# Per-pair starting steps and work splits in a four-layer image network kernel

## The chip, the cores and the metric

The kernel runs on one core of one Trainium2 chip. Such a core has TensorE (PE, matmuls into PSUM), VectorE (DVE), ScalarE (ACT, table functions), GpSimd (POOL, elementwise, SBUF only) and SyncE (SP, which here issues all DMAs). Each engine runs its own queue strictly in the order in which it was written; engines wait for each other through semaphores. The metric is the device time of one execution in microseconds (us).

## The reference

The input is x of shape (8, 384, 32, 32) in fp32. Four residual layers follow one another, each with a group norm (32 groups) ahead:

```python
x = x + L0(gn(x))   # Mamba: in_proj 384->2x768, causal conv 3, silu, x_proj, dt_proj + softplus,
                    #   h = exp(dt*A)*h + dt*u*B ; y = sum_n h*C + D*u   (16 states, 1024 positions)
                    #   y * silu(z), out_proj 768->384
x = x + L1(gn(x))   # 1x1 matmul, 8x8 FFT filter, 3x3 depthwise, gelu(x1)*x2, 1x1 matmul
x = x + L2(gn(x))   # layer norm over channels, Mamba as in L0, then MLP 384->1536 gelu ->384
x = x + L3(gn(x))   # 3x3 depthwise convolution
```

The scan is the heart: for 768 channels and 16 states a first-order recurrence over 1024 positions, in two layers and eight images.

## The kernel before

An image of 1024 positions is cut into two chunks of 512. There are 32 chunks: 0 to 15 belong to layer 0 (two per image), 16 to 31 to layer 2. Even chunks begin an image, odd ones end it. A chunk has 24 steps (NQ): six groups of 128 channels, each in four substeps. In a step 128 partitions hold 16 states times 8 channels, and four blocks j of 512 positions make 32 channels. All the work is counted in steps; the step at which chunk n begins is `s["t"] = 24 n`.

What one step does, by process (lines of the kernel before):

- `begins` (777): SP loads g, the product dt*u spread over the states (1 MB in SBUF, tag g, five buffers), and every fourth step dts. The load for step t waits until PE has gathered step t-5.
- `times` (800): POOL multiplies g (128x2048) by B.
- `decays` (810) and `exps` (825): PE spreads dt into the PSUM tiles dA, ACT turns each into exp(dt*A).
- `scans` (833): DVE runs four scans. SHARE says how many of the four blocks are scanned into dA rather than into g. For these DVE also makes the product with C (`g<-dA,bc`); for the others POOL does it in `states` (881), `g<-g,bc` on 128x1024 at a share of 2.
- `carries` (859): in even chunks only, ACT copies the last column of each block, the state with which the odd chunk starts. POOL's C product and PE's next dA wait for that.
- `gathers` (894): PE sums over the states into y; `gatings` (917): DVE multiplies y by silu(z).

Around the steps run jobs of whole chunks, which use PE, ACT and DVE between them: `front` (621) makes the next chunk's u, B, C and dt (blocks of in_proj with the convolution on DVE, a Silu, `step` for dt and its softplus, `scaled` for dt*u on POOL); `gates` (575) makes z in two halves; `finish` (937) makes out_proj, in layer 2 followed by `mlp` (1201). `layer1` (1069) and `layer3` (1266) do the convolution layers of an image while later chunks scan; they are added once the image's odd chunk has ended. In `layer3` PE does TAPS (4) of the nine taps of each block by diagonal matrices and DVE the other five (`ps_dw<-xp,vec,ps_dw`).

All 32 chunks are one program, unrolled in Python. The order on each queue is made by `Order` (194), a list scheduler: processes are generators that name the engine they need next; `Clocks` (68) estimates when the engine is free and the operands are there; the process that can begin earliest goes next. Among those that can begin at once the scan's processes go first on PE, ACT and SP; after that the lower `due`, a step, wins on PE, POOL and SP, and on DVE and ACT the one ready longest. So `due` is a preference. A hard floor is `pace(t)` (292): the process may not go on before the written scans reach step t. Conv blocks of `front` are paced at `s["t"] - 18 + d`, dt at `s["t"] - 9 + 3*d`, layer 1's patches at steps 8, 13, 18 and 23 of the even chunk after the image, its depthwise sums at 28 and 38, layer 3's taps at 20 and every 7 from there.

ACT needs another table for Silu and Gelu than for Exp and Ln. Such calls are gathered: `session` (563) holds them until LEAD (2) exponentials more than scans are written, or until PATIENCE (6.0) has passed on the scheduler's clock. A session is a table load, the function, a table load back.

Every recorded operation has line 189 in the profile, so groups are told apart by tile names.

Of the kernel before, what the change touches and what calls it, by code (L numbers as in the profile page):

```python
# [19 lines left out]
KC = C // P  # L20
# [26 lines left out]
NBANK = 3  # L47
LEAD = 2
PATIENCE = 6.0
TAPS, LAST_TAPS = 4, 5  # L50
SHARE = (2, 2, 2, 2)
SET_EXP = "natural_log_exp_and_others"
# [11 lines left out]
def _img(ap):  # L64
    return ap.rearrange("p (h w) -> p h w", w=W)


# [182 lines left out]
def tile_conv_preact_d4(ctx: ExitStack, tc: tile.TileContext, a: dict, out: bass.AP):  # L250
# [41 lines left out]
    def pace(t):  # L292

        return once(lambda: ahead["scans"] >= 4 * min(t, len(steps)))
# [268 lines left out]
    def session():  # L563

        asked = []

        def ready():
            asked.append(order.now)
            late = order.now - asked[0] > PATIENCE
            late = late or ("begin", ahead["decays"] // 4) not in said  # L570
            return 0.0 if ahead["decays"] - ahead["scans"] >= LEAD or late or order.stuck else None

        return ready

    def gates(s, h):
        n = s["n"]
        yield once(lambda: "normed" in s and "loaded" in s["w"] and (n == 0 or chunks[n - 1]["gated"] >= (NH if h == 0 else ND)))
        z = s["z", h] = new(wk, [P, NH, T], F32, "z", 2)

        def block(d):  # L580
            ps, tag = yield from projection(s, "ps_z", "z", (h * NH + d) * P)
            yield on("ACT", ps)
            act(z[:, d, :], ps, AF.Copy)
            ps_give(ps, tag)

        yield from together(s["t"] + (6 if h else -4), [block(d) for d in range(NH)])
        yield on("ACT", z, when=session())
        act(_flat(z), _flat(z), AF.Silu)
        exp_set()
        s["gates", h] = True  # L590
# [30 lines left out]
    def front(s):  # L621
        c, n, due = s["c"], s["n"], s["t"] - 26
        yield once(lambda: n == 0 or "normed" in chunks[n - 1] and (n == 1 or ("gates", 1) in chunks[n - 2]))
# [21 lines left out]
        def block(d):  # L645
            if n not in (0, B * NCH - 1, B * NCH):
                yield pace(s["t"] - 18 + d)
            ps, tag = yield from projection(s, "ps_in", "in", d * P)
            yield on("ACT", ps)
            act(u[d], ps, AF.Identity, scale=vec[:, d, 2:3], bias=vec[:, d, 3:4])  # L650
            if c < NCH - 1:
                act(s["xt"][:, d, :], ps[:, T - 2 : T], AF.Copy)
            for j in (1, 2):
                yield on("DVE", u[d])
                vector.scalar_tensor_tensor(
                    u[d][:, j:T], ps[:, 0 : T - j], vec[:, d, 2 - j : 3 - j],
                    u[d][:, j:T], ALU.mult, ALU.add,
                )
            ps_give(ps, tag)
# [38 lines left out]
        def step(d):  # L698
            if n not in (0, B * NCH - 1, B * NCH):
                yield pace(s["t"] - 9 + 3 * d)  # L700
            ps, tag = yield from chain(
# [26 lines left out]
            else:  # L728
                yield on("POOL", pc[:, 0, :])
                gpsimd.tensor_sub(m, v, pc[:, 0, :])  # L730
                rest, tag = m, None
            order.add(scaled(d, v), s["t"] - 14)
            yield on("ACT", rest)
# [31 lines left out]

    ahead = {"decays": 0, "scans": 0}
    said = {}

    def seen(*keys):


        def ready():
            return None if any(k not in said for k in keys) else 0.0

        return ready

    def begins():
# [32 lines left out]
    def decays():  # L810
        for t, (s, i) in enumerate(steps):
            k, sub = QUADS[i]
            for j in range(4):
                procs["decays"]["due"] = t - 2
                yield on("PE", when=lambda: (
                    None if ("begin", t) not in said or t > 0 and (
                        ("scan" if j < 4 - SHARE[(i - 1) % NSUB] else "product", t - 1, j) not in said
                        or j > 0 and not carried(t - 1, j)
                    )
                    else max(clocks.known(s["dts"][k]), clocks.last.get(dAs[j].name, 0.0))  # L820
                ))
                mm(dAs[j], selr[:, j, :], s["dts"][k][:, sub, :])
                said["decay", t, j] = True
# [9 lines left out]
    def scans():  # L833
        for t, (s, i) in enumerate(steps):
            for j in range(4):
# [4 lines left out]
                g = s["g", i]  # L840
                low = 4 - SHARE[i % NSUB]
                q = 4 * i + j
# [16 lines left out]
    def carries():  # L859
        for t, (s, i) in enumerate(steps):  # L860
            if s["c"] == NCH - 1:
                continue
            low = 4 - SHARE[i % NSUB]
            yield on("ACT", when=lambda: (
# [11 lines left out]
    def carried(t, j):  # L876
        s, i = steps[t]
        low = 4 - SHARE[i % NSUB]
        return s["c"] == NCH - 1 or ("carry", t, j) in said or 0 < j < low

    def states():
        for t, (s, i) in enumerate(steps):
            low = 4 - SHARE[i % NSUB]
            procs["states"]["due"] = t + 0.3
# [52 lines left out]
    def finish(s):  # L937
        n, t = s["n"], s["t"]
        last = s["pre"] == "l2_"
        due = t + NQ + (10 if not last else 23 if s["c"] == 0 else 16)  # L940
        end = n == len(chunks) - 1
# [50 lines left out]

        yield from together(t + NQ + 6, [block(m) for m in range(KC)])
        s["free"] = True
# [73 lines left out]

    def layer1(s):
        b, due = s["b"], s["t"] + (NQ + 14 if s["n"] == B * NCH - 1 else 3 * NQ - 14)  # L1070
        x = [chunks[s["n"] - 1]["x"], s["x"]]
# [9 lines left out]
        for hb in range(H // PS):  # L1081
            if not hurry:
                yield pace(s["t"] + NQ + 8 + 5 * hb)
            xl = new(p1, [P, KC, 2, P], F32, "xl")
# [38 lines left out]
        for hf in range(2):  # L1123
# [22 lines left out]
            if not hurry:  # L1146
                yield pace(s["t"] + NQ + 28 + 10 * hf)
            yield from depthwise(p1, P, "ps_dw", due, [some(0), some(2)])
# [117 lines left out]
    def layer3(s):  # L1266
        b, due = s["b"], s["t"] + 3 * NQ - 1
        x = [chunks[s["n"] - 1]["x"], s["x"]]
# [22 lines left out]
        taken = [0]  # L1291
        taps = LAST_TAPS if end else TAPS
        for k in range(KC):
# [7 lines left out]
            for hf in range(2):  # L1301
                yield pace(s["t"] + NQ + 20 + (7 if b < B - 2 else 4) * (2 * k + hf))
                rows = slice(hf * 512, (hf + 1) * 512)
# [31 lines left out]
    chunks = [  # L1335
        {"pre": pre, "src": src, "b": b, "c": c, "n": (q * B + b) * NCH + c, "gated": 0}
        for q, (pre, src) in enumerate((("l0_", a["x"]), ("l2_", x_mid)))
# [7 lines left out]
    def start_jobs(t):  # L1345
        n, i = divmod(t, NQ)
        if i or n >= len(chunks):
            return
        s = chunks[n]
        order.add(gates(s, 1), t + 8)  # L1350
        if s["c"] == 0 and n + NCH < len(chunks):
            m = chunks[n + NCH]
            order.add(measured(m), t + NQ + 4)
        if n + 1 < len(chunks):
            later = chunks[n + 1]
            order.add(front(later), t + NQ - 26)
            order.add(gates(later, 0), t + NQ - 4)
        order.add(finish(s), t + NQ + 10)
# [178 lines left out]
```

## Time and profile before

| | us |
|---|---|
| median of 3 runs (6209.75 to 6211.98) | 6210.31 |
| profiled execution | 6204.07 |
| its span, first to last instruction | 6202.2 |
| start to the first scan | 74.4 |
| layer 0, odd chunks 5, 7, 9, 11, 13 | 169.3 each |
| layer 0, even chunks 4, 6, 8, 10, 12 | 185.3 to 192.6 |
| layer 2, chunks 20 to 29, odd / even | 198.3 to 199.4 / 187.0 to 188.4 |
| chunk 17, the longest | 218.4 |
| after the last scan | 120.7 |

A chunk's time is from its first scan to the next chunk's first scan. In a group's line the engine stands first, then the operation, the tile written and those read, shapes, the count, and behind the bar the busy time, the mean of one in ns, and the engine's idle time ahead of these instructions with what ended it. An fp32 matmul is recorded as two passes, so its count is doubled. Records of matmuls overlap: their pace is the distance of their starts, not their length.

### The profile page before, as it was taken

How to read it: one execution, taken by the hardware profiler on the slowest of the kernel's cores; microseconds unless marked ns; L12 is line 12 of the kernel's file. 1: busy time of each engine (PE TensorE's matmuls, PEld its weight loads, DVE VectorE, ACT ScalarE, POOL GpSimd, SP SyncE). 2: the span in 40 equal slices, each digit the busy share in tenths (PEclk: the TensorE clock that was granted, in tenths of full speed). 3: DMA queues.
4: the chain of work that ended last, by engine and by line, in shares of the span. 5: the costliest groups of instructions: out<-in, count | busy, mean ns of one | idle time of the engine just before them, and what ended most of it. 6: DMA issues, size and time to landing. Idle time of an engine off the chain costs nothing.

```text
span 6202.2 us, 62614 instructions
## 1 busy us (share of the span) xinstructions
PE 5799.2 (94%) x19022; PEld 2184.1 (35%) x19022; DVE 5616.8 (91%) x6381; ACT 4241.3 (68%) x7942; POOL 5725.3 (92%) x2028
## 2 busy tenths in 40 slices
PE   6878999999999999999989999999999999999998
PEld 2223333333333333333333333333333333333333
DVE  5999999999998999998887899899998999989994
ACT  5656677677667767776676676777767777677753
POOL 4999999999999999989997999999999999999991
PEclk8889999999999999999999999999999999999999
DMA  6877878877887888787777888878888788888871
GB/s 178 193 184 186 195 190 194 204 188 193 190 193 185 196 205 189 192 205 186 180 185 183 199 196 219 200 198 209 198 215 201 200 207 198 212 205 197 207 197 58
DMA packets 346724, 1195.88 MB, mean 193 GB/s; under 512 B 40516, under 2 KB 142580, under 8 KB 248084
## 3 DMA queue, kind: packets, MB, share of 16 engines
q1 hardware_dynamic: 346388, 1191.88, 79.1%
q8 instruction: 152, 2.49, 0.2%
q14 instruction: 184, 1.51, 0.1%
HBM read 1040.73 MB, written 150.99 MB: 192 GB/s over the span
## 4 chain that ended last, share of the span: by engine, by line
DVE 25%; PE 13%; POOL 8%; DMA 4%; issue 4%; ACT 4%; SPq 0%; POOLq 0%; DVEq 0%; ACTq 0%
DVE g L189 11%; DVE dA L189 8%; POOL g L189 6%; DVE u L189 2%; PE ps_dn L189 2%; PE ps_up L189 2%; PE ps_dw L189 2%; PE y L189 2%; PE dA L189 2%; DMA g<-dud 2%; DVE ps_dw L189 1%; PE ps_z L189 1%; DMA dts<-dtd 1%; PE ps_out L189 1%; DVE st L189 1%
## 5 line engine op out<-in xcount | busy, mean ns | idle before, releaser
L189 POOL TENSOR_TENSOR g<-g,bc 128x1024 f32<-128x1024 f32 (+1 forms) x1536 | 5243.4, 3447 | 248.1 <-ACT carry L189 94.1
L189 ACT ACTIVATE dA<-dA,w_A 128x512 f32<-128x512 f32 x3072 | 2018.6, 661 | 931.0 <-PE dA L189 919.4
L189 PE MATMUL dA<-dts,selr 96*128 96x512 bf16 x3072 | 1190.0, 390 | 233.2 <-DVE g L189 207.6
L189 DVE TENSOR_TENSOR_SCAN g<-dA,carry,g 128x512 f32<-128x512 f32 x768 | 955.4, 1269 | 75.1 <-POOL g L189 61.1
L189 DVE TENSOR_TENSOR g<-dA,bc 128x512 f32<-128x512 f32 x1536 | 994.5, 677 | 17.3 <-ACT carry L189 16.4
L189 DVE TENSOR_TENSOR_SCAN g<-dA,g 128x512 f32<-128x512 f32 x768 | 909.4, 1209 | 85.7 <-POOL g L189 77.8
L189 DVE TENSOR_TENSOR_SCAN dA<-dA,carry,g 128x512 f32<-128x512 f32 x768 | 952.2, 1271 | 28.0 <-ACT dA L189 27.4
L189 DVE TENSOR_TENSOR_SCAN dA<-dA,g 128x512 f32<-128x512 f32 x768 | 909.0, 1212 | 62.3 <-ACT dA L189 61.7
L189 PE MATMUL y<-g,sely 128*32 128x512 f32 x6144 | 857.0, 627 | 38.0 <-POOL g L189 35.6
L189 PEld LDWEIGHTS <-selr 96*128 96x128 bf16 x3072 | 300.2, 98 | 1113.0 <-issue 1072.0
L189 PE MATMUL ps_in<-xf,w_in 128*128 128x512 f32 x1152 | 562.7, 610 | 10.0 <-ACT xf L189 7.6
L189 PE MATMUL ps_z<-xf,w_z 128*128 128x512 f32 x1152 | 567.8, 597 | 3.6 <-DVE dt L189 3.6
L189 PE MATMUL ps_up<-t,mw 128*128 128x512 f32 x1152 | 556.0, 596 | 7.1 <-DVE u L189 5.2
L189 PE MATMUL ps_out<-u,w_out 128*128 128x512 f32 x1152 | 547.5, 594 | 0.4 <-ACT carry L189 0.4
L189 PE MATMUL ps_dn<-h,mw 128*128 128x512 f32 x1152 | 545.3, 594 | 1.6 <-ACT h L189 1.6
L189 PE MATMUL ps_dw<-tp,diag 128*128 128x512 f32 x864 | 438.8, 609 | 9.6 <-ACT diag L189 9.6
L189 PEld LDWEIGHTS y<-g,sely 128*32 128x32 f32 x6144 | 126.3, 109 | 599.2 <-issue 313.0
L189 PEld LDWEIGHTS ps_in<-xf,w_in 128*128 128x128 f32 x1152 | 218.6, 195 | 263.8 <-issue 234.2
L189 POOL TENSOR_TENSOR dt<-dt,u 128x512 f32<-128x512 f32 x192 | 244.3, 1274 | 72.4 <-PE ps_dr L189 56.3
L189 PEld LDWEIGHTS ps_dn<-h,mw 128*128 128x128 f32 x1152 | 217.8, 190 | 259.9 <-issue 235.3
L189 PEld LDWEIGHTS ps_up<-t,mw 128*128 128x128 f32 x1152 | 214.4, 190 | 267.2 <-issue 230.4
L189 PEld LDWEIGHTS ps_z<-xf,w_z 128*128 128x128 f32 x1152 | 215.9, 191 | 252.7 <-issue 215.2
(118 smaller groups left out, 6451.1 us busy)
## 6 DMA issues: line engine op xcount, KB each, us to landing
g<-dud SPq DMA_DIRECT2D x768, 1024.0 KB, 8.2
dtd<-pc SPq DMA_DIRECT2D x192, 384.0 KB, 4.0
dts<-dtd SPq DMA_DIRECT2D x192, 384.0 KB, 7.8
mw<-in_l_mlp_w SPq DMA_DIRECT2D x192, 384.0 KB, 6.5
dud<-dt SPq DMA_DIRECT2D x768, 64.0 KB, 3.2
xf<-in_x SPq DMA_DIRECT2D x16, 768.0 KB, 9.1
x<-in_x SPq DMA_DIRECT2D x16, 768.0 KB, 11.9
x_mid<-x SPq DMA_DIRECT2D x16, 768.0 KB, 7.0
```

The source lines that it names most:

```text
L189: return call(out_, *args, **kw)
```

## The change

The constants LEAD, PATIENCE, TAPS and SHARE and the numbers in the paces and dues become a table WAYS of 18 named values with alternatives, the first of each being the value of before. CHOICE holds one number per chunk, the same for both chunks of a pair, which `ways` turns into one alternative for every name. When a chunk's first step comes up, `start_jobs` puts that chunk's values into `way`. `front` of the next chunk, `finish` of this one and the layers added during it read a copy; sessions read it as it stands; the share stays with the chunk, since its scans, carries and C products must agree.

Decoded, what differs from before:

| chunks | values |
|---|---|
| 0, 1 | share (2,2,2,3), out 2, begin -24 |
| 2, 3 | out 2, begin -28 |
| 4 to 7 | patch_every 4, out 2, begin -28 |
| 8, 9 | the same, lead 1 |
| 10, 11 | the same, lead 2, dt_every 2.5, early -1 |
| 12, 13 | patch_every 4, out 2, begin -28, lead 3 |
| 14, 15 | patch_every 4, out 10, begin -28, lead 3 |
| 16, 17 | share (2,3,2,2) |
| 18, 19 | dt_every 2.5, wait 9 |
| 20, 21 | dt -10, dt_every 2.5, wait 9 |
| 22, 23 | lead 3, wait 4, share (2,3,2,2) |
| 24, 25 | dt -10, dt_every 2.5, taps 3, wait 9, share (2,2,2,1) |
| 26, 27 | dt -8, dt_every 2.5, taps 3, wait 9, share (2,2,2,1) |
| 28, 29 | as before |
| 30, 31 | dt -10, taps 3, wait 9, share (2,2,2,1) |

(A value "tap" is also set in chunks 2 to 15, where no layer 3 reads it.) "out" is the due of out_proj, 6 before; "begin" that of `front`, -26 before. "early" is the due of the first half of z, -4 before; "lead" and "wait" stand for LEAD and PATIENCE. Share 3 in a substep leaves POOL a C product of 128x512 there, share 1 one of 128x1536. Taps 3 leaves PE three taps and gives DVE six; layer 3 of an image reads it when it is added, in the even chunk after the image, so it reaches three images. Operations are otherwise the same in kind and number; conv, patch and sums starts other than patch_every keep their values.

```diff
-LEAD = 2
-PATIENCE = 6.0
-TAPS, LAST_TAPS = 4, 5
-SHARE = (2, 2, 2, 2)
+LAST_TAPS = 5
+WAYS = {
+    "lead": (2, 1, 3),
+    "conv": (-18, -20, -16),
+    "dt": (-9, -10, -8),
+    "dt_every": (3, 2.5, 2),
+    "patch": (8, 5, 11),
+    "patch_every": (5, 4),
...
+    "out": (6, 2, 10),
+    "mlp": (0, -6, 6),
+    "wait": (6.0, 4.0, 9.0),
+    "begin": (-26, -24, -28),
+    "scaled": (-14, -18, -10),
+    "share": ((2, 2, 2, 2), (2, 2, 2, 3), (2, 3, 2, 2), (2, 2, 2, 1)),
+}
+CHOICE = (
+    96013674, 96013674, 19490544, 19490544, 19495161, 19495161, 19495161, 19495161, 19495162,
...
+def ways(number):
+
+    chosen = {}
+    for name, values in WAYS.items():
+        number, digit = divmod(number, len(values))
+        chosen[name] = values[digit]
+    return chosen
...
-            late = order.now - asked[0] > PATIENCE
+            late = order.now - asked[0] > way["wait"]
...
-                yield pace(s["t"] - 18 + d)
+                yield pace(s["t"] + o["conv"] + d)
...
-                yield pace(s["t"] - 9 + 3 * d)
+                yield pace(s["t"] + o["dt"] + o["dt_every"] * d)
...
+    def share(t):
+        s, i = steps[t]
+        return s["share"][i % NSUB]
...
-                low = 4 - SHARE[i % NSUB]
+                low = 4 - share(t)
...
-        yield from together(t + NQ + 6, [block(m) for m in range(KC)])
+        yield from together(t + NQ + o["out"], [block(m) for m in range(KC)])
...
-                yield pace(s["t"] + NQ + 8 + 5 * hb)
+                yield pace(s["t"] + NQ + o["patch"] + o["patch_every"] * hb)
...
-        taps = LAST_TAPS if end else TAPS
+        taps = LAST_TAPS if end else o["taps"]
...
+        way.update(ways(CHOICE[n]))
         s = chunks[n]
+        s["share"] = way["share"]
...
-            order.add(front(later), t + NQ - 26)
+            order.add(front(later), t + NQ + way["begin"])
```

## The prediction

> **What bounds the kernel now.** I read the totals first, then stretches of the span cut at the first scan of each chunk (VectorE runs 96 scans per chunk, so the cuts are exact), then GpSimd's waits in one stretch, then prices by form of instruction.
>
> ```profile
> PE 5799.2 (94%) x19022; PEld 2184.1 (35%) x19022; DVE 5616.8 (91%) x6381; ACT 4241.3 (68%) x7942; POOL 5725.3 (92%) x2028
> ```
>
> Three engines are over 90% busy, so no single one can be relieved alone. The stretches show which binds where. Columns: us, then busy us of PE, weight loads, DVE, ACT, POOL, then the granted clock, DMA share, GB/s. The five are chunks 9 and 10 (layer 0), then 25, 26 and 30 (layer 2).
>
> ```profile
> 1696.00:1865.30 169.30, 164.50 (x561) 61.78 (x558) 164.95 (x181) 116.51 (x211) 168.64 (x54) 1.00 0.82 196
> 1865.30:2057.90 192.60, 175.37 (x603) 66.55 (x602) 173.09 (x206) 136.94 (x297) 176.49 (x63) 0.95 0.79 189
> ...
> 4729.80:4928.60 198.80, 193.13 (x620) 72.84 (x618) 188.48 (x214) 137.56 (x220) 187.01 (x69) 1.00 0.82 202
> 4928.60:5115.60 187.00, 182.86 (x599) 69.30 (x600) 175.09 (x202) 137.41 (x267) 182.93 (x71) 1.00 0.85 207
> ...
> 5700.30:5884.60 184.30, 177.47 (x583) 66.88 (x584) 172.02 (x195) 134.39 (x259) 182.65 (x71) 1.00 0.85 205
> ```
>
> Odd chunks of layer 0 are POOL and nothing else: 169.30 - 168.64 = 0.66 us idle. Even ones have 192.60 - 176.49 = 16.1 us of POOL idle: the largest stock of waits that repeats (12.0 to 16.1 us in chunks 4 to 12). Layer 2 is bound by PE: 4.1 us idle in chunk 26, 5.7 in chunk 25, while POOL has 4.1 and 11.8. What POOL waits for in chunk 10, and its worst wait:
>
> ```profile
> POOL g L189 <- ACT carry L189: 7.6, 4, 3.0
> POOL g L189 <- DMA g<-dud: 5.9, 4, 4.0
> POOL dt L189 <- ACT z L189: 1.2, 1, 1.2
> POOL g L189 <- DVE g L189: 1.0, 1, 1.0
> ```
> ```profile
> 1971.14 2.36 POOL L189 TENSOR_TENSOR g<-g,bc 128x1024 f32<-128x1024 f32 x1
> 1977.54 6.84 POOL L189 TENSOR_TENSOR g<-g,bc 128x2048 f32<-128x2048 f32 x2 [4.04 <-DMA g<-dud]
> ```
>
> A load of g may go out only when PE has gathered the step five before. Going through POOL's written order, I count by how many steps its B product (128x2048) runs ahead of its C product (128x1024) at each issue. Of 768 issues 88 stand three ahead; these hold 49.6 of the 76.8 us that POOL waits for g in the whole run. In chunks 6, 8, 10 and 12 the waits of 4.0 to 4.5 us sit at such places, steps 15 and 16.
>
> One table session of ScalarE (Silu or Gelu between the Exps) blocks that engine for 4.1 us; after this one POOL waited 3.0 us for a carry:
>
> ```profile
> 1920.10 1.28 ACT L189 ACT_TABLE_LOAD   x1
> 1921.39 1.49 ACT L189 ACTIVATE z<-z 128x1536 f32<-128x1536 f32 x1
> 1922.89 1.28 ACT L370 ACT_TABLE_LOAD   x1
> ```
>
> **Prices.** In the groups by form the mean ns stands after the busy time; the line of the timeline below them gives PE's pace.
>
> ```profile
> L189 POOL TENSOR_TENSOR g<-g,bc 128x2048 f32<-128x2048 f32 x768 | 3479.6, 4535 | 90.5 <-DMA g<-dud 76.5 <-PE dA L189 3.3 <-PE ps_dn L189 3.1
> ...
> L189 POOL TENSOR_TENSOR g<-g,bc 128x1024 f32<-128x1024 f32 x768 | 1810.9, 2359 | 157.7 <-ACT carry L189 94.1 <-DVE g L189 59.2 <-PE dA L189 3.1
> ...
> L189 DVE TENSOR_TENSOR g<-dA,bc 128x512 f32<-128x512 f32 x1536 | 994.5, 677 | 17.3 <-ACT carry L189 16.4
> ...
> L189 DVE SCALAR_TENSOR_TENSOR ps_dw<-xp,vec,ps_dw 128x512 f32<-128x512 f32 x210 | 154.9, 738 | 14.1 <-PE ps_dw L189 13.7
> ```
> ```profile
> 3360.94 5.31 PE L189 MATMUL ps_dn<-h,mw 128*128 128x512 f32 x12
> ```
>
> A C product of one block moved from DVE to POOL costs POOL (4535 - 2359)/2 = 1.09 us and frees 0.68 of DVE. An fp32 matmul is two passes; twelve took 5.31 us, the last recorded as 0.59, so a pass is (5.31 - 0.59)/11 = 0.43 and a matmul 0.86 us.
>
> **The change part by part.** No transfer is added; 36 blocks go from POOL to DVE and 36 back, 18 matmuls go from PE, 18 operations come to DVE. The rest is order. The sum is made against the profiled execution: 6204.1 us, span 6202.2 and 1.9 around it. The median of the runs stands 6.2 above it.
>
> *Chunks 0 and 1, share 3 in every fourth step.* Twelve blocks leave POOL: -13.1 us; DVE gets 12 x 0.68 = +8.1. POOL idles 15.4 and 5.0 us in these chunks, DVE 28.1 and 12.8, PE more. Between -13.1 (POOL binds throughout) and +8.1 (DVE does), POOL is nearest to full, but part of its idle time is the start's: **-8**.
>
> *Chunks 2 and 3.* POOL idles 9.1 us, of which waits for g 6.5, at steps 7, 8, 15 and 17. Bounds 0 and -9.1; the order is milder but not free of threes: **-3**.
>
> *Chunks 4 to 13: out-projection four steps earlier in the order of preference, patches every 4 steps instead of 5, front two steps earlier, lead 1 or 3 in some.* The written orders show three things. Threes on POOL fall from 30 to 8, and those at steps 13 to 16, where the 4 us waits are, become twos (not in chunk 12). In chunks 6 to 13 one z session per pair leaves the even chunk (5 to 4) for the odd one (3 to 4), where no carry stands behind it. And in chunks 6 to 9 twelve patch matmuls move from the odd to the even chunk and three z matmuls back; at 0.86 us or less each that is under 8 us for PE, which idles 17 there. Per pair that is up to 5.1 us of g waits and about 3.0 of carry wait. What is late next: three ahead means DVE's scans were behind, so part of the freed time becomes waiting for scans. SP issues the same loads in another order; xf goes out two steps earlier on the same queue as g, covered only if g is not late. Bounds per pair: 0, and -14.4 (all POOL idle of chunks 4 to 13 is 72 us in five pairs). I take -5, about the g waits alone: **-25**.
>
> *Chunks 14 and 15.* POOL idles 26.9 us, PE 33.9, DVE 48.6: nobody binds. Two sessions leave, one joins chunk 16. Bounds 0 and -27; as a pair before it: **-5**.
>
> *Chunks 16 to 19.* Shares take 13.1 us off POOL, add 8.1 to DVE. Ten matmuls, 8.6 us, leave chunk 17's part of PE's queue, eight of them down-projections to chunk 18; 17 is the longest chunk (218.4 us), 18 has 8.7 us of PE idle. Bounds -8.6 and +8.1; PE binds more than DVE there: **-5**.
>
> *Chunks 20 to 23.* PE idles 5 us a chunk and its work is the same; dt starts one step earlier, every 2.5. Bounds 0 and -10 a pair: **-3** for both.
>
> *Chunks 24 to 31, share 1 and three taps.* The taps apply to three images: 18 matmuls off PE, -15.5 us; 18 x 0.738 = +13.3 on DVE, from which 36 products, 24.4 us, go; POOL gets 36 x 1.09 = +39.2, 13.1 a pair. In chunks 25 and 26 POOL works 369.9 of 385.8 us; with 13.1 more it needs 383.0. So relief of 5.2 us on PE is worth at most 385.8 - 383.0 = 2.8, and with POOL's present waits kept (15.9) the pair gets 13.1 longer. Chunk 30 alone, at 182.65 busy, would need 189.2 against 184.3. Ends for three pairs: -15.5 and +39; with waits halfway between the odd layer-0 chunks' 0.66 and today's the pair is near even, and the tail behind the last scan keeps its work: **0**.
>
> A rule to weigh: the Trainium skill, Perfetto Trace Analysis, section Identifying the Most-Contended Engine, says that matmul busy share tells little of TensorE's headroom and that the weight loads' busy share should be read. In chunk 26 that is 69.30/187.0 = 37%, so by it PE would have room, the 18 matmuls would be worth nothing, and the sum would be 13 us higher. The trace's gapless passes 0.43 us apart speak for PE being full, and I keep them.
>
> Sum: -8 - 3 - 25 - 5 - 5 - 3 + 0 = -49. 6204.1 - 49 = 6155; on the median 6210.3 - 49 = **6161 us**.
>
> **The rivals.**
>
> *The waits only change their name.* With POOL no longer ahead it waits for scans; DVE idles 16.5 to 19.5 us in chunks 6 to 12, partly for other reasons (a dA product of PE comes 4.2 us late for ScalarE at 1935.1 us). Then pairs give -1 instead of -5 and the rest half: -5 - 12 = -17, about 6193. For it: carry waits, 7.6 us in chunk 10, exceed the g waits.
>
> *New load waits (slower).* Every engine's queue is fixed when the program is written, and the real landing of g (median 8.2 us, a chain piece of 15.79 at 5498.86) is not in it. If the new order puts one wait of 4.0 us into each chunk that lacks one: eleven chunks now have a wait for g of 2.5 us or more, so 21 would gain 4.0 = +84, against -49, which gives 6245. It cancels the gain at 12 new waits and decides from 16. Against it: threes fall from 88 to 64.
>
> *Nearly all goes.* Both the g and carry waits leave the five pairs (-13 each) and the rest stands: -49 - 40 = -89, 6121. Against it: even chunks still keep four sessions.
>
> *The shares overload POOL.* If the pairs 24 to 27 and 30/31 pay the whole 39, the sum is -10: 6200, no change.
>
> **How the numbers follow.** No change means within 0.2%, 12.4 us. Forecast (-30 to -70) 0.42; name only (-13 to -30) 0.16; nearly all 0.10; shares, or gains that cancel, within 12 us: 0.11; new load waits 0.21. Faster 0.42 + 0.16 + 0.10 = 0.68, same 0.11, slower 0.21. The low end, 6118, cuts half of "nearly all"; the high end, 6240, cuts about half of the slow case. With gain alone the range would be 6140 to 6180.
>
> **What would show it.** Right: even chunks 6 to 12 about 185 us instead of 189 to 193, with no 4 us wait for g at step 15; odd ones still near 169; chunk 17 shorter; chunk 24 and 30 not shorter, POOL at full there. Wrong: new waits of POOL for g or carry in odd chunks of layer 0, or pairs of 24 to 31 longer by over 6 us.

## The result, and the profile after

The median went from 6210.86 us (six runs, 6204.84 to 6213.29) to 6179.53 us (six runs, 6168.05 to 6182.48): a ratio of 0.9948 with a 95% interval of 0.9935 to 0.9961, so 31 us or half a per cent faster. The profiled execution after took 6178.5 us with a span of 6176.7, 25.5 less than the span before.

The totals of the page after differ little from those of before. PE has 18 matmuls fewer (36 records) and is busy 24.7 us less, DVE is busy 13.6 us more, POOL 3.1 us less:

```profile
PE 5774.5 (93%) x18986; PEld 2186.5 (35%) x18986; DVE 5630.4 (91%) x6399; ACT 4232.4 (69%) x7924; POOL 5722.2 (93%) x2028
```

POOL's idle time fell by 22.4 us and DVE's by 39.1; PE's stayed (403.0 and 402.2). So what was gained is idle time of POOL and DVE between their instructions. Cut at the first scan of each chunk, the difference of the two spans comes out like this (us):

| chunks | before | after | difference | term of the prediction |
|---|---|---|---|---|
| start | 74.4 | 73.5 | -0.9 | |
| 0, 1 | 364.5 | 375.6 | +11.1 | -8 |
| 2, 3 | 354.3 | 348.7 | -5.6 | -3 |
| 4 to 13 | 1793.1 | 1783.6 | -9.5 | -25 |
| 14, 15 | 392.3 | 367.0 | -25.3 | -5 |
| 16 to 19 | 791.6 | 787.0 | -4.6 | -5 |
| 20 to 23 | 772.0 | 768.6 | -3.4 | -3 |
| 24 to 31 and the tail | 1660.0 | 1672.6 | +12.6 | 0 |

In chunks whose order was the same in several of the kernels below, a pair's time differs by 2 to 5 us from one execution to the next, so the single pairs are read no finer than that. Chunks 4 to 13 together took 1793.1 to 1800.1 us in the five profiles that have the order of before there (mean 1796.3), and 1781.1 to 1783.6 in the three that have the order of the change (mean 1782.3): by the means they gained 14.0 us, not 9.5. For chunks 0 and 1 and for 14 and 15 the means differ from the table by 1.1 us at most.

Stretches of the span after, one per line. The columns are us, then busy us of PE, weight loads, DVE, ACT and POOL, then granted clock, DMA share, GB/s. They are chunks 0 and 1, 7 and 8, 14 and 15:

```profile
73.50:267.80 194.30, 145.57 (x428) 43.38 (x427) 163.13 (x186) 113.07 (x233) 170.41 (x61) 0.79 0.82 194
267.80:449.10 181.30, 144.54 (x456) 45.75 (x455) 167.61 (x185) 104.70 (x163) 169.87 (x57) 0.85 0.81 188
1337.00:1515.10 178.10, 169.86 (x552) 62.08 (x553) 164.18 (x180) 120.36 (x206) 175.67 (x56) 0.96 0.79 189
1515.10:1695.30 180.20, 168.86 (x608) 67.93 (x607) 172.98 (x207) 134.03 (x302) 169.21 (x61) 0.98 0.83 198
2581.40:2765.80 184.40, 171.26 (x591) 66.63 (x589) 174.72 (x207) 137.27 (x296) 177.30 (x64) 0.96 0.87 208
2765.80:2948.50 182.70, 171.93 (x590) 66.32 (x591) 167.72 (x181) 130.53 (x237) 179.06 (x63) 1.00 0.83 193
```

The same view of the kernel before, for its chunks 7 and 8:

```profile
1337.10:1506.40 169.30, 164.49 (x561) 61.78 (x558) 164.95 (x182) 116.50 (x211) 168.64 (x54) 1.00 0.82 196
1506.40:1696.00 189.60, 172.30 (x603) 65.45 (x602) 172.85 (x205) 136.80 (x297) 176.42 (x63) 0.96 0.79 190
```

The even chunk 8 became 9.4 us shorter, and the odd chunk 7 8.8 us longer. POOL's busy time went the same way: 168.64 to 175.67 in chunk 7, 176.42 to 169.21 in chunk 8. Its idle time in the two was 0.66 + 13.18 = 13.8 us and is now 2.43 + 10.99 = 13.4. Work was moved across the cut, and little else happened.

What POOL waited for in chunks 4 to 13, before and then after (us in total, times, longest):

```profile
POOL g L189 <- ACT carry L189: 32.7, 17, 3.8
POOL g L189 <- DMA g<-dud: 24.9, 16, 4.5
POOL g L189 <- DVE g L189: 3.8, 6, 1.0
```
```profile
POOL g L221 <- ACT carry L221: 47.0, 25, 3.9
...
POOL g L221 <- DVE g L221: 2.3, 4, 0.7
POOL g L221 <- DMA g<-dud: 1.7, 2, 1.5
```

The waits for g did go, nearly all of them (24.9 to 1.7 us). Waits for carries rose by 14.3, and the ten chunks gained 9.5 (14.0 by the means). Over the whole run the same exchange shows: POOL's waits for g fell from 76.8 to 52.6 us, and its waits for carries rose from 94.1 to 118.8.

### The profile page after: what moved, and what is told of

The parts are those of the page before. It is cut to its first block, busy times and chain, and to the rows that moved or that the text cites. A ratio compares the mean times of both kernels' runs of the same rounds, so it can differ in the third digit from the quotient of the medians.

```text
span 6176.7 us, 62588 instructions
## 1 busy us (share of the span) xinstructions
PE 5774.5 (93%) x18986; PEld 2186.5 (35%) x18986; DVE 5630.4 (91%) x6399; ACT 4232.4 (69%) x7924; POOL 5722.2 (93%) x2028
## 3 DMA queue, kind: packets, MB, share of 16 engines
HBM read 1040.73 MB, written 150.99 MB: 193 GB/s over the span
## 4 chain that ended last, share of the span: by engine, by line
DVE 19%; PE 18%; POOL 17%; issue 8%; ACT 7%; DMA 4%; SPq 0%; POOLq 0%; DVEq 0%; ACTq 0%
POOL g L221 15%; DVE g L221 9%; DVE dA L221 6%; DMA g<-dud 3%; PE y L221 3%; PE ps_dw L221 3%; PE ps_dn L221 2%; PE dA L221 2%; PE ps_up L221 2%; ACT dA L221 2%; DVE u L221 1%; PE ps_in L221 1%; PE ps_z L221 1%; POOL dt L221 1%; DVE ps_dw L221 1%
## 5 line engine op out<-in xcount | busy, mean ns | idle before, releaser
L221 POOL TENSOR_TENSOR g<-g,bc 128x2048 f32<-128x2048 f32 (+3 forms) x1536 | 5241.8, 3448 | 241.5 <-ACT carry L221 118.8
L221 DVE TENSOR_TENSOR g<-dA,bc 128x512 f32<-128x512 f32 x1536 | 994.7, 679 | 16.9 <-ACT carry L221 15.7
L221 DVE SCALAR_TENSOR_TENSOR u<-ps_in,w_vec,u 128x511 f32<-128x511 f32 (+1 forms) x384 | 279.8, 732 | 28.8 <-ACT xt L221 17.0
## 6 DMA issues: line engine op xcount, KB each, us to landing
x<-in_x SPq DMA_DIRECT2D x16, 768.0 KB, 11.7
```

The costliest lines, as they stand in the source:

```text
L221: return call(out_, *args, **kw)
```

## The experiments

### Parts of the change alone

Four kernels take a part of the change back or make a part alone. CHOICE holds one number per chunk; zero means the values of before. First, chunks 0 and 1 back to zero:

```diff
 CHOICE = (
-    96013674, 96013674, 19490544, 19490544, 19495161, 19495161, 19495161, 19495161, 19495162,
...
+    0, 0, 19490544, 19490544, 19495161, 19495161, 19495161, 19495161, 19495162, 19495162,
...
```

> The changed kernel with the values of before in chunks 0 and 1 (share 2,2,2,2, out 6, begin -26). Theory 'each pair answers for itself': in the two profiles chunks 0 and 1 grew from 364.5 to 375.6 us, so 11 us come back, about 6168 us (ratio to before 0.993). Rival, the prediction's term: share 3 there saves 8 us, so 6187 (0.996). Third: the pair's loss is paid back by chunks 2 and 3, which got 5.6 shorter, so only 5 to 6 us come back, 6174.

Measured: 6190.25 us against 6207.13, ratio 0.9973 [0.9963, 0.9984]. Chunks 0 and 1 took 364.8 us again, as before the change. But the pair behind them, whose values were left alone, went from 348.7 to 377.0, nearly all of it in one step: the last of chunk 3 took 33.1 us, where most last steps take 6 to 8. POOL's queue around it:

```profile
784.56 2.35 POOL L221 TENSOR_TENSOR g<-g,bc 128x1024 f32<-128x1024 f32 x1 [2.48 <-PE ps_dw L221]
786.87 2.50 POOL L221 TENSOR_TENSOR dt<-dt,u 128x512 f32<-128x512 f32 x2
789.34 1.26 POOL L221 TENSOR_TENSOR gate<-gate,other 64x512 f32<-64x512 f32 x1
805.98 1.27 POOL L221 TENSOR_TENSOR dt<-dt,u 128x512 f32<-128x512 f32 x1 [15.38 <-PE ps_dr L221]
810.53 4.53 POOL L221 TENSOR_TENSOR g<-g,bc 128x2048 f32<-128x2048 f32 x1 [3.29 <-DMA g<-dud]
```

The first B product of chunk 4 stands at 810.53, behind the products dt*u of that chunk; one of these waited 15.38 us for PE's ps_dr, the tile that dt goes through. All the work on ps_dr in this neighbourhood lies from 785.2 us on, while depthwise sums of layer 1 (ps_dw) had begun at 760.6; 7.99 us of these stand in PE's queue directly ahead of that ps_dr. Whatever the three values cost in chunks 0 and 1, they happened to keep this collision away. The total lies near the rival's 6187 us, but not for its reason: the pair itself gave back 10.8 us, and the next one took 28.3.

Second, chunks 24 to 31 back to zero:

```diff
 CHOICE = (
...
-    6377319, 6377319, 6377328, 6377328, 175375532, 175375532, 264660570, 264660570, 264660579,
-    264660579, 0, 0, 264660543, 264660543,
...
+    6377328, 6377328, 175375532, 175375532, 0, 0, 0, 0, 0, 0,
+    0, 0,
```

> The changed kernel with the values of before in chunks 24 to 31 (no three taps, no share 1, dt and wait as before). Theory 'each pair answers for itself': these pairs and the tail went from 1660.0 to 1672.6 us together, so about 12.6 us come back, 6167 us (0.993). Rival, the prediction's term: share and taps cancel, no change, 6179.5 (0.995).

Measured: 6197.37 us, ratio 0.9981 [0.9973, 0.9990]. Chunks 24 and 25 came back to 387.2 from 390.5, but the last step of chunk 30 took 34.8 us and the pair 30, 31 went to 409.2. Chunks 24 to 31 and the tail took 1690.8 us, 18.2 more than with the change, so neither expectation was met.

Third, the values of 14 and 15 alone, all others zero:

```diff
 CHOICE = (
...
+    0, 0, 0, 0, 19849457, 19849457, 0, 0, 0, 0,
...
```

> The kernel before with new values in chunks 14 and 15 alone (patch_every 4, out 10, begin -28, lead 3). Theory 'each pair answers for itself': the pair went from 392.3 to 367.1 us, so 6186 us (0.996). Rival, the prediction's term of 5 us: 6206 (0.999). Third: the gain needs the pairs ahead to arrive in another state; then also near 6206.

Measured: 6248.65 us, ratio 1.0066 [1.0054, 1.0079]. The pair itself went from 392.3 to 376.5, which is 15.8 of its 25 us. Chunks 24 to 27, which got no values, lost 31 us, and the tail 9.6. None of the three expectations covers this total.

Fourth, the values of 4 to 13 alone:

```diff
 CHOICE = (
...
+    0, 0, 0, 0, 19495161, 19495161, 19495161, 19495161, 19495162, 19495162,
+    19731384, 19731384, 19495163, 19495163, 0, 0, 0, 0, 0, 0,
...
```

> The kernel before with new values in chunks 4 to 13 alone. Theory 'the waits only change their name': the five pairs went from 1793.1 to 1783.5 us, so 6201 us (0.9985), with GpSimd's waits for g near 2 us in these chunks and its waits for carries grown to about 47. Rival, the prediction's term of 25 us: 6186 (0.996).

Measured: 6271.12 us, ratio 1.0102 [1.0087, 1.0117]. Chunks 4 to 13 took 1790.9 us, 2 less than in the profile before and 5 less than the mean; POOL waited 8.5 us for g there and 42.3 for carries. The total is far from both expectations. Pair 22, 23 went from 386.7 to 424.1, because the last step of chunk 22 took 41.8, and chunks 28 to 31 lost another 27 us. POOL at the long step:

```profile
4345.28 2.35 POOL L221 TENSOR_TENSOR g<-g,bc 128x1024 f32<-128x1024 f32 x1 [7.24 <-ACT carry L221]
4353.76 1.15 POOL L221 TENSOR_TENSOR spm<-dt,pc 128x512 f32<-128x512 f32 x1 [6.14 <-ACT pc L221]
4356.89 1.16 POOL L221 TENSOR_TENSOR spm<-dt,pc 128x512 f32<-128x512 f32 x1 [1.98 <-ACT pc L221]
...
4367.94 1.15 POOL L221 TENSOR_TENSOR spm<-dt,pc 128x512 f32<-128x512 f32 x1 [4.96 <-ACT pc L221]
...
4373.89 4.52 POOL L221 TENSOR_TENSOR g<-g,bc 128x2048 f32<-128x2048 f32 x1
```

Here the softplus of the next chunk's dt (spm, pc) stands ahead of the scan: the next B product starts 28.6 us after the last C product began.

A fifth kernel adds to the fourth one single value, "gate" 10, in chunks 20 and 21:

```diff
 CHOICE = (
     0, 0, 0, 0, 19495161, 19495161, 19495161, 19495161, 19495162, 19495162,
     19731384, 19731384, 19495163, 19495163, 0, 0, 0, 0, 0, 0,
-    0, 0, 0, 0, 0, 0, 0, 0, 0, 0,
+    78732, 78732, 0, 0, 0, 0, 0, 0, 0, 0,
     0, 0,
 )
```

> The earlier run with new values in chunks 4 to 13 alone, and one preference more: gate 10 instead of 6 in chunks 20 and 21. That run was 64 us slower than before, 41.8 us of it in one long step at the end of chunk 22, where the next chunk's dt came late. Theory 'the total is decided by long steps at chunk ends, and any small value may set or clear one': the long step is gone and 15 to 30 us with it, about 6245 us. Rival 'the loss comes from the values in chunks 4 to 13 themselves': still near 6271.

Measured: 6243.31 us against 6206.86, ratio 1.0058 [1.0043, 1.0074], 28 us less than without the value. The last step of chunk 22 is 6.0 us again, the pair 390.8. But pair 20, 21 got 9.4 us longer, and chunks 24 to 31 with the tail still took 31 us more than before. So the long step came and went with the order alone, and without it 28 of the 64 us came back, not the larger part of the loss.

What follows from these five: a value set in one pair rewrites the order of everything behind it, and a part taken alone is not the part's share of the whole. Longest are the steps at a chunk's end at which the next chunk's dt is late. The change has one of 31.8 us (end of chunk 17; 40.4 before), in which POOL waits 9.4 us for ScalarE's part of the next dt.

### What the engines' work is worth, in the order of before

The other way to find what binds is to leave the order of every queue as it was, and to take single instructions out of it. The scheduler's clocks are told of the instruction, but it is not issued.

```diff
-            mm(_img(ps[:rows]), made[q], rhs, start=t == 0, stop=t == count - 1)
+            if pool is p2 and t == 1 and count == TAPS:
+                clocks.op("PE", "matmul", _img(ps[:rows]), [made[q], rhs])
+            else:
+                mm(_img(ps[:rows]), made[q], rhs, start=t == 0, stop=t == count - 1)
```

> The kernel before in its own order, with the second of four taps left out of TensorE's depthwise matmuls in layer 3 for images 0 to 6 (that tap is missing in the output): 42 fp32 matmuls less, 36 us of TensorE at 0.86 each, nothing added elsewhere. Theory 'TensorE binds layer 2': 20 to 36 us faster, 6171 to 6187. Rival 'TensorE has room there, GpSimd and the order bind': 0 to 8 us, above 6199.

Measured: 6209.50 us against 6206.86, ratio 1.0006 [0.9997, 1.0015]. Taking 36 us off PE (by the distance of its passes; its busy time on the page fell by 21.9), in the layer that I had called bound by PE, gained nothing. Chunks 25 and 26 of this kernel:

```profile
4736.10:4934.50 198.40, 190.20 (x611) 71.31 (x610) 188.45 (x214) 137.53 (x220) 186.82 (x68) 1.00 0.83 203
4934.50:5121.50 187.00, 181.52 (x595) 68.51 (x596) 175.19 (x203) 137.40 (x267) 182.98 (x71) 1.00 0.84 209
```

They last 198.4 and 187.0 us, 198.8 and 187.0 before; PE's idle time rose from 5.7 to 8.2 and from 4.1 to 5.5.

```diff
+            if t <= AHEAD:
                 g = s["g", i] = new(wk, [P, 4, T], F32, "g", AHEAD + 1)
+                kept.append(g)
                 sync.dma_start(_flat(g), src)
+            else:
+                g = s["g", i] = kept[t % (AHEAD + 1)]
...
+                clocks.op("SP", "dma_start", _flat(g), [src])
```

> The kernel before in its own order; from step 5 on g is not loaded, the five buffers stay and their old contents are multiplied on (the spread of dt*u is left out, so the values are other ones). This takes GpSimd's 76.8 us of waits for g and 800 MB of transfers. Theory of the prediction 'the waits for g are time': 30 to 77 us faster, and chunks 6 to 12 about 5 us each. Rival 'they only change their name': under 15 us, chunks 6 to 12 as before, waits for carries grown in their place.

Measured: 6204.98 us against 6208.19, ratio 0.9997 [0.9987, 1.0007]. Its transfers fell to a quarter:

```profile
HBM read 240.67 MB, written 150.99 MB: 63 GB/s over the span
```

against 1040.73 MB of reads before. POOL's waits over the whole run, of the kernel before and then of this one:

```profile
POOL g L189 <- ACT carry L189: 94.1, 54, 7.1
POOL g L189 <- DMA g<-dud: 76.8, 45, 6.3
POOL g L189 <- DVE g L189: 60.2, 46, 4.2
...
POOL g L189 <- PE dA L189: 6.4, 5, 3.1
```
```profile
POOL g L189 <- ACT carry L189: 132.4, 62, 7.6
POOL g L189 <- DVE g L189: 77.2, 52, 5.0
...
POOL g L189 <- PE dA L189: 18.1, 5, 3.6
POOL g L189 <- DMA g<-dud: 8.4, 2, 6.7
```

The waits for g fell by 68.4 us; those for carries, scans and dA rose by 38.3 + 17.0 + 11.7 = 67.0. This is a change of name, to within 1.4 us.

```diff
-            act(carry[:, 4 * i : 4 * i + low].unsqueeze(2), g[:, 0:low, T - 1 : T], AF.Copy)
+            clocks.op("ACT", "activation", carry[:, 4 * i : 4 * i + low].unsqueeze(2), [g[:, 0:low, T - 1 : T]])
...
-                act(carry[:, q : q + 1], dAs[j][:, T - 1 : T], AF.Copy)
+                clocks.op("ACT", "activation", carry[:, q : q + 1], [dAs[j][:, T - 1 : T]])
```

> The kernel before in its own order without ScalarE's carry copies (odd chunks start from zero states, so the values are other ones); 1152 small operations, 212 us, less on ScalarE, and GpSimd's C products and TensorE's dA products wait for the scans alone. Theory 'the way over ScalarE is what GpSimd's 94 us of waits for carries are': 40 us or more faster, in even chunks of both layers. Rival 'behind them the scans are late, ScalarE only stands last': under 20 us, with the waits now named after VectorE.

Measured: 6189.48 us against 6208.19, ratio 0.9968 [0.9955, 0.9981]: 19 us, from 212 us of copies left out (the sum of their records, which overlap others; ScalarE's busy time fell by 118). The largest waits of POOL now carry the name that stood third:

```profile
POOL g L189 <- DVE g L189: 129.6, 90, 4.2
POOL g L189 <- DMA g<-dud: 89.1, 52, 8.3
```

Of the 94.1 us of waits for carries, 69.4 came back under the scans' name and 12.3 under that of the loads of g. That is the rival's account, at the edge of its 20 us.

```diff
     def exp_set():
-        nc.scalar.preload_act_table_set(SET_EXP)
+        if act_set["now"] is None:
+            nc.scalar.preload_act_table_set(SET_EXP)
...
             act_set["now"] = func
+            func = AF.Identity
```

> The kernel before in its own order, without ScalarE's 288 table loads after the first (Silu and Gelu are left out: Identity in their place, so the values are other ones). 287 x 1.283 = 368 us less on ScalarE. Theory 'sessions cause the waits for carries': GpSimd's 94 us of such waits fall to less than half and the time by 40 to 90 us, 6120 to 6170. Rival 'ScalarE at 68% has room, the carries wait for scans': under 15 us, above 6192.

Measured: 6165.91 us against 6206.86, ratio 0.9935 [0.9922, 0.9949]: 41 us, from 367 us of table loads (two of the 288 stay). The time is at the near end of the first theory's range and outside the rival's, but the theory's mechanism is not what the profile shows: POOL's waits for carries fell from 94.1 to 78.9 us, not to less than half. The gain is spread thin, 1 to 4 us in most pairs, 5 in chunks 4 and 5, 7 in 14 and 15, none in 0 to 3. What else the loads held up is not shown.

```diff
-                        vector.scalar_tensor_tensor(
-                            _img(ps), window(t // 3, t % 3), dw3[:, k, t : t + 1], _img(ps),
...
+                        if t == 5 and taps == TAPS:
+                            clocks.op("DVE", "scalar_tensor_tensor", _img(ps), ins)
+                        else:
+                            vector.scalar_tensor_tensor(_img(ps), *ins, ALU.mult, ALU.add)
```

> The kernel before in its own order, without one of the five taps that VectorE adds in layer 3, images 0 to 6 (missing in the output): 42 x 0.738 = 31 us less on VectorE, all of it in layer 2, to be set beside the 36 us taken from TensorE that brought nothing. Theory 'VectorE carries the chain of layer 2' (it has over half of the chain of chunks 25 and 26): 12 to 25 us faster. Rival 'no single engine binds there': under 8 us.

Measured: 6193.51 us against 6208.19, ratio 0.9978 [0.9968, 0.9988]: 15 us from 31 us of DVE (26.5 by its busy time), as the first theory has it. The same two chunks as above, now 2.1 and 0.3 us shorter than before the change:

```profile
4726.80:4923.50 196.70, 192.93 (x618) 72.91 (x617) 185.58 (x209) 137.63 (x221) 186.72 (x68) 1.00 0.83 205
4923.50:5110.20 186.70, 182.51 (x599) 69.40 (x600) 174.08 (x200) 137.59 (x267) 182.87 (x71) 1.00 0.87 210
```

PE is as full in them as before, at 192.93 of 196.70 us, and yet they are shorter.

```diff
-                gpsimd.tensor_sub(m, v, pc[:, 0, :])
+                if d % 3 == 0:
+                    clocks.op("POOL", "tensor_sub", m, [v, pc[:, 0, :]])
+                else:
+                    gpsimd.tensor_sub(m, v, pc[:, 0, :])
```

> The kernel before in its own order, without 32 of GpSimd's 96 products spm in layer 2 (the rest of dt's split is another value there): 32 x 1.16 = 37 us less on GpSimd, in layer 2. Theory 'GpSimd binds the even chunks of layer 2' (4.1 us idle): 10 to 20 us faster, even chunks two thirds of it. Rival 'no single engine binds there': under 8 us.

Measured: 6203.82 us against 6208.19, ratio 0.9992 [0.9983, 1.0001]: 4 us from 37 us of POOL, within what can be told from nothing.

Per microsecond left out, then: DVE 0.47, POOL 0.12, table loads 0.11, carries 0.09, PE and the loads of g nothing. Against what fell in the engines' busy times on the pages (DVE 26.5 us, POOL 34.6, ScalarE 365.1 and 118.1) they are 0.55, 0.13, 0.11 and 0.16. Where instructions were left out matters too: those of DVE, PE and POOL lie in layer 2 only, the carries in the even chunks of both layers. From layer 0 nothing was taken off PE, DVE or POOL. Its odd chunks 5 to 13 took 169.1 to 169.3 us in all six of these kernels, with POOL busy for 168.64 of 169.30 before, so that POOL binds there stands untested. These are prices in a fixed order; what a scheduler would put into the freed time is not in them.

### A further version

The clocks give an end of their own when the last instruction is written. A further version takes the change and alters values by which that end comes out earlier: wait 9 in 14 and 15; tap 16 in 22 and 23; dt -8 and gate 10 in 24 and 25; dt -8, tap 16 and early -7 in 28 and 29; share (2,2,2,3) for (2,2,2,1) in 30 and 31.

```diff
 CHOICE = (
...
-    19495162, 19731384, 19731384, 19495163, 19495163, 19849457, 19849457, 172186884, 172186884,
-    6377319, 6377319, 6377328, 6377328, 175375532, 175375532, 264660570, 264660570, 264660579,
-    264660579, 0, 0, 264660543, 264660543,
...
+    19731384, 19731384, 19495163, 19495163, 26226749, 26226749, 172186884, 172186884, 6377319, 6377319,
+    6377328, 6377328, 175379906, 175379906, 264739311, 264739311, 264660579, 264660579, 122490, 122490,
+    92473659, 92473659,
```

> The changed kernel with values altered in chunks 14/15 (wait 9), 22/23 (tap 16), 24/25 (dt -8, gate 10), 28/29 (dt -8, tap 16, early -7) and 30/31 (share 2,2,2,3 instead of 2,2,2,1), found by searching on the kernel's own clocks, which put it 7.5 us under the changed kernel. Theory 'the clocks carry over to the chip': about 6172 us. Rival 'differences this small on the clocks are lost on the chip': 6179 plus or minus 10. If share 1 in 30/31 was the cause of the 11.6 us by which that pair grew, about 6168.

Measured: 6167.83 us against 6206.86, ratio 0.9939 [0.9927, 0.9951]. That is 39.0 us under the kernel before, where the change is 31.3 under it. The two were timed in different jobs and their intervals overlap, so the step from the one to the other is likely and not settled. Pair 30, 31, which got another share, took 386.0 instead of 392.8, and 24, 25 384.5 instead of 390.5, each in one profile.

How the clocks' own end stood to the chip, as the difference to the kernel before in us:

| kernel | clocks | chip |
|---|---|---|
| further version | -51.7 | -39.0 |
| the change | -44.2 | -31.3 |
| last pairs back | -22.9 | -9.8 |
| first pair back | -20.6 | -16.9 |
| only 14 and 15 | +14.0 | +41.5 |
| long step cured | +21.3 | +36.5 |
| only 4 to 13 | +40.1 | +64.0 |

Every version whose order is new is worse on the chip than on the clocks, by 4 to 28 us, 16 on average. Two neighbours change places in two cases, and the rest of the ranking holds.

## Why the prediction was right or wrong

**The total** was right in sign: -31 where the sum said -49, at the near end of the forecast's own bracket (-30 to -70), on the side of the rival in which the waits only change their name (-17); the interval of the measurement, 24 to 40 us, reaches out of the bracket. But the sum came this near for partly wrong reasons. Four of its terms were off by 13 to 20 us: chunks 0 and 1, 4 to 13, and 24 to 31 gave 47 us less than forecast together, and 14 and 15 gave 20 more. That the 20 makes up for part of the 47 is luck. Two of the signs that the prediction named for being wrong did come: pair 30, 31 got 11.6 us longer, and POOL had new waits for g, up to 3.1 us, in the odd chunk 1.

**Chunks 0 and 1: wrong in sign** (-8, measured +11.1; -10.8 when undone). I took the end of the range where POOL binds. But POOL lost only 3.9 of the 13.1 us in these two chunks (chunk 2 has 9.3 us less instead), and it got idle time: 15.4 us in chunk 0 before, 194.30 - 170.41 = 23.9 after. What POOL waited for in the two chunks after; the longest wait, of 8.3 us, is over at 69.01 us, ahead of the first scan at 73.54, and belongs to the start, where the kernel before has one of 6.3:

```profile
POOL g L221 <- ACT carry L221: 17.3, 7, 5.3
POOL g L221 <- DMA g<-dud: 17.2, 8, 8.3
POOL g L221 <- DVE g L221: 5.0, 4, 2.4
```

So within the chunks the waits for g are 8.9 us, against 2.1 before; those for carries rose from 12.4 to 17.3 and those for scans from 0.7 to 5.0. The rival of new load waits came up here (and in chunk 22, where waits for g went from 2.4 to 7.9 us and the chunk got 2.9 us shorter all the same), but loads are 6.8 of 16.0 us of new waits. That any of these is the cause and not one more name isn't shown; +8.1, the bound for the case that DVE sets the pace, is near the measurement as well. The share, out and begin of this pair were taken back together only, so that the share is what costs isn't shown either. With the three left as they were, the long step at the end of chunk 3 costs more than that.

**Chunks 4 to 13: the step that failed is "I take -5, about the g waits alone".** The places and counts were right: the waits for g in these chunks fell from 24.9 to 1.7 us. Their worth was not: the kernel without loads of g gained nothing that can be told from noise, 8 us at most by its interval. I had counted a wait that ended last as time that the chunk would get back, and on the whole something else was hardly earlier. The rival "The waits only change their name", which gave -1 a pair, describes what happened to the waits; in time a pair gained 1.9 us by the two profiles and 2.8 by the means, between that rival and the forecast's 5. Where these 1.9 to 2.8 us come from is not shown. Even chunks 10 and 12 became 184.8 and 184.6 us, with odd ones at 170, as forecast; chunks 6 and 8 went to 180, but only since their odd neighbours took the work.

**Chunks 14 and 15: mis-sized** (-5, measured -25.3). It was bounded by POOL's idle time, 26.9, and I set it like its neighbours, against the row that said that nobody binds there. Nearly all of the bound came out. Leaving out every table load gains 7 here, so the two sessions that leave are not enough to explain it, and the values alone give 15.8. Which value does it stays open.

**Chunks 16 to 23: about right** (-8, measured -8.0; chunk 17 went from 218.4 to 205.8, as said, and its last step is the part of this that shows: 40.4 to 31.8 us). These sums are within what pairs differ by on their own, so that they fit is little evidence. The term for 20 to 23 had also left out the share (2,3,2,2) of chunks 22 and 23, which takes twelve blocks, 13.1 us, off POOL.

**Chunks 24 to 31: "Layer 2 is bound by PE" failed.** The rows did not single PE out: in chunk 26 POOL was idle for 4.07 us and PE for 4.14. Nor does 0 follow from the working that it ends: 383.0 us of POOL's work and halfway waits of (15.9 + 1.3)/2 = 8.6 make 391.6 against 385.8, 5.8 longer a pair and 17 for three. Measured are +4.1, -1.2 and +11.6 for the three pairs, 14.5 together. The relief of PE is worth nothing, as the kernel with fewer taps shows in the order of before. The Trainium skill (Perfetto Trace Analysis, section Identifying the Most-Contended Engine) says that the busy share of matmuls tells little of TensorE's headroom. This case agrees: PE was busy for 182.86 of 187.0 us in chunk 26, its weight loads for 69.30, and 36 us less of matmuls gained at most 0.03%, the near end of the interval. By that rule the prediction put this part at +13, without a working; measured is +12.6 with the tail. The agreement is partly chance. Chunk 30, said to need 189.2 us, took 188.8, but POOL worked 183.71 of them, 1.1 more than before and not 6.5; chunk 26 did not change, and 31, with 7.1 more, was not foreseen. In chunk 25 POOL reached what I had named as its limit:

```profile
4698.20:4894.60 196.40, 185.17 (x597) 68.99 (x596) 188.41 (x212) 132.80 (x209) 195.88 (x68) 0.99 0.82 196
```

195.88 of 196.40 us. The chunk is 2.4 us shorter than its namesake before, but now POOL's work alone fills it. Which of the values of 24 to 31 makes the sum longer was not tested one by one.

**What sets the pace instead, in layer 2.** Of what was left out, only DVE gave back about half. In the chain of waits of chunks 25 and 26 before, DVE's scans and products hold the largest shares:

```profile
by line: DVE g L189 25.5%; DVE dA L189 17.4%; POOL g L189 6.2%; issue 5.8%; DVE u L189 4.7%; DMA g<-dud 4.0%; PE ps_z L189 2.7%; DMA mw<-in_l_mlp_w 2.5%; PE ps_up L189 2.4%; DVE ps_dw L189 2.3%; DMA xf<-x_mid 1.9%; DVE st L189 1.8%; PE dA L
```

I had read only busy shares of stretches, in which DVE stood behind PE and POOL (175.09 of 187.0). The chain and the runs agree on DVE for this order: the taps (ps_dw) hold 2.3% of 387 us of it, 8.9 us, of some 22 us of taps in the two chunks (30 of 0.738), which would be a price of 0.40, an estimate; the run gave 0.47. In the changed kernel, where share 1 gives POOL more to do, the chain of the same two chunks has another head:

```profile
by line: POOL g L221 27.5%; issue 13.1%; DVE g L221 11.2%; DVE dA L221 7.0%; PE ps_in L221 4.1%; PE ps_up L221 2.8%; PE y L221 2.5%; PE dA L221 2.4%; POOL dt L221 2.3%; DVE ps_dw L221 2.3%; DMA g<-dud 2.1%; POOL spm L221 2.1%; ACT dA L221 2
```

So there POOL stands first and DVE behind it. No run took work off an engine in that order.

**Still open:** which value made 14 and 15 faster, the largest single part of the gain; which of three values slows chunks 0 and 1, and by what wait; what binds layer 0, where no work was left out; which engine binds layer 2 in the new order; and why new orders do worse on the chip than on the scheduler's clocks.

## What to carry to other kernels

When three engines are over 90% busy, neither busy shares nor the name of a wait told here what is worth removing: take 30 to 40 us of one engine's instructions out of an unchanged order and time it, engine by engine, before pricing an edit. A wait that ends last is worth only its lead over the one that ends second, so price it by leaving it out, not by its sum. Where a list scheduler writes the order, a local value has remote costs: compare whole versions, look at each chunk's last step for a late first operand of the next chunk, and don't add up parts.

## What the runs showed that was not expected

- An engine without gaps need not be the bound: PE was busy for 98% of chunk 26 (182.86 of 187.0 us), and leaving out 42 fp32 matmuls gave a ratio of 1.0006 [0.9997, 1.0015].
- Reads from HBM of 1040.73 MB or of 240.67 MB make no difference to this kernel, although the queues were busy for 79% of the span in the one case and 21% in the other.
- The granted clock in chunks 0 and 1 was 0.79 and 0.85 where later stretches have 0.96 to 1.00; the kernel before has 0.80 and 0.86 there, so the clock is not what makes the two chunks 11 us longer.
